# First attention of a fused transformer kernel: output product, shift and two routing calls moved between the two halves of the score rounds

## The chip, the cores and the metric

The kernel runs on one core of one Trainium2 chip. The metric is the device time of one execution in microseconds (us); of several runs the median is taken. A core has five engines that run their own queues and meet at semaphores: TensorE (PE; its weight loads are shown as PEld), VectorE (DVE), ScalarE (ACT), GpSimd (POOL) and SyncE (SP), which issues DMAs here.

## The reference

Two layers, each an attention and a mixture of experts, on x of 64 sequences with 128 rows of 128 numbers, in fp32:

```python
x = x + xattn0(layernorm(x), fside, ctx, ctx)   # 16 heads of 8; 128 + 120 keys
x = x + ffn0(layernorm(x))                       # 8 experts, 2 for each row, logits from a small attention
x = x + xattn1(layernorm(x), ctx, ctx)           # 16 heads; 120 keys
x = x + ffn1(layernorm(x))                       # 8 experts, 2 for each row
```

The first attention is what the change is about. For each sequence and head:

```python
q = (xn @ Wq + bq); k = concat(fside @ Wk + bk, ctx); v = concat(fside @ Wv + bv, ctx)
attn = softmax(q @ k.T * 8 ** -0.5)
out = concat_heads(attn @ v) @ Wp + bp
```

## The kernel before

`attention` (L232 on) is a loop over `it`, one turn for each sequence with five turns to drain (L517). It is a software pipeline: in turn `it`, the score maxima are made for sequence `it`, the exponentials for `it - 2`, the products with the values for `it - 3`, and the output steps for `it - 3` to `it - 5`. Sequences come in groups of four (`GB`); once a group, spread over the four turns, the next group's queries, keys and values are prepared (`prep`).

The steps of a turn of the first attention, with their engines:

- `rounds(0, 1)` and `rounds(2, 3)` (L524, `round_` L413). A round is two banks of maxima (`max_bank`: TensorE at L373, then a DVE reduction at L385) and two banks of scores (`score_bank`: TensorE at L401, then an ACT exponential at L409). Two rounds are one block: eight banks of PSUM[...].
- `shift` (L426): two TensorE transposes of the negated maxima (L430), and two DVE operations that add them to the queries (L433). The scores of a sequence (two turns after its maxima) need its queries shifted.
- `values` (L437): 64 TensorE records at L446, then `out1`, an ACT copy (L455).
- `out2` (L458): two transposes (L462), a DVE reciprocal and product. `out3` (L473): a transpose (L475) and an ACT copy. `out4` (L480): the output product (L482). `out5` (L485): a DVE addition to x (L487) and `aside.made`, the statistics of the next norm (L109).
- `aside.ahead` (L547): the statistics of the first norm for a later sequence, on DVE; with every fourth one POOL makes the roots.
- `aside.call`: one step of the router of the experts (`Router.call`, L612) and of its lists, twice in a turn. The router has three generators: `front` (normed rows on POOL, transposes at L176, logits at L652), `back` (the choice of experts, on DVE, POOL and ACT; ranks by TensorE at L805), `sent` (scatters by POOL, L783). Each says at which call it goes on; most of `back` takes one step in each call, 15 or 16 calls for two groups of sequences.
- `prep(it, half)` (L323), by `it % 4`: turn 0 writes the next group's queries (`prep_q`, a product at L289 and four ACT writes at L293, two in each half); turn 2 its keys (`prep_k`, L202, two ACT writes at L207) and values (`prep_v`, L214, two DVE additions at L221); turn 3 turns the normed rows (`prep_x`, L176).

Every engine of `ORDERED` takes its instructions in the order in which the program writes them (`manual_schedule`). The order of the calls in L540 to L556 is therefore the order on TensorE, DVE, ACT and POOL each. SP's DMAs are not held to it inside this loop.

All PSUM banks come from one pool of eight (`mtile`, L275). A bank goes back when its last reader is done, and the one that has been free longest is handed out next. So about eight banks after a bank is taken, TensorE waits for that bank's reader. `prep_q(g, 0)` takes a bank that `prep_q(g, 1)` reads too; it is not handed out in between.

Of the kernel before, what the change touches and what calls it, by code (L numbers as in the profile page):

```python
# [44 lines left out]
def transformer_kernel(ctx, tc, a, out):  # L45
# [155 lines left out]
    def keys_of(w, src, g, n0, pk):  # L201
        nc.tensor.matmul(  # L202
            pk[:, : GB * n0], lhsT=w["wk"], rhs=src.rearrange("d b k -> d (b k)"),
            start=True, stop=True,
        )
        for v in range(NV):
            nc.scalar.activation(  # L207
                K2[g % 2][:, v, :, 0:n0], pk[:, : GB * n0].rearrange("p (b k) -> p b k", b=GB),
                AF.Identity, bias=w["bk"][:, v : v + 1], scale=kmask[:, v : v + 1],
            )  # L210

    def values_of(w, src, g, n0, pv):
        for j in range(GB):
            nc.tensor.matmul(  # L214
                pv[:n0, j * D : (j + 1) * D], lhsT=src[:, j, :], rhs=w["wv"],
                start=True, stop=True,
            )
        pv5 = pv[:n0, :].rearrange("k (b h i d) -> k b h i d", b=GB, i=2, d=HD)
        bv5 = w["bv"][:n0, :].rearrange("k (h i d) -> k h i d", i=2, d=HD)
        for i in range(2):  # L220
            nc.vector.tensor_tensor(  # L221
                VS[g % 2][0][:n0, :, :, i, 16 * i : 16 * i + HD], pv5[:, :, :, i, :],
                bv5[:, :, i, :].unsqueeze(1).to_broadcast([n0, GB, H // 2, HD]),
                ALU.add,
            )
# [6 lines left out]
    def attention(layer, w, norm, first, aside):  # L232
# [5 lines left out]
        with ExitStack() as es:  # L238
# [13 lines left out]
            def loads(g):  # L252
                n = KF if first else KC
                t = work.tile([D, GB, n], F32, name="kvT", tag="kvT")
                nc.sync.dma_start(t, a["fsideT" if first else "ctxT"][:, g * GB : (g + 1) * GB, :])
                src[g] = t
# [13 lines left out]
            def context(g):  # L270
                if first:
                    context_k(g)
                    context_v(g)

            def mtile():  # L275
                return banks.tile([128, 512], F32, name="bank", tag="bank")

            def prep_x(g):
                xnT = work.tile([D, GB * S], F32, name="xnT", tag="xnT", bufs=1)
                norm.turned(normed.pop(g), mtile(), xnT)  # L280
                xnTs[g] = xnT
                q4s[g] = work.tile([128, GB, NS, S], F32, name="q4", tag="q4", bufs=3)
# [3 lines left out]
            def prep_q(g, v):  # L286
                if v == 0:
                    pqs[g] = mtile()
                    nc.tensor.matmul(pqs[g], lhsT=w["wq"], rhs=xnTs[g], start=True, stop=True)  # L289
                pq = pqs[g]  # L290
                for i in range(2):
                    s = 2 * v + i
                    nc.scalar.activation(  # L293
                        q4s[g][:, :, s, :], pq.rearrange("p (b q) -> p b q", b=GB),
                        AF.Identity, bias=w["bq"][:, s : s + 1], scale=hmask[:, s : s + 1],
                    )

            def prep_k(g):
                keys_of(w, src[g], g, n0, mtile())

            def prep_v(g):
                values_of(w, src[g], g, n0, mtile())
# [20 lines left out]
            def prep(it, half):  # L323

                g, j = it // GB + 1, it % GB
                if not first:
                    if g == 1:
                        if (j, half) == (2, 1):
                            prep_v(1)
                        elif (j, half) == (1, 0):  # L330
                            prep_k(1)
                    elif g < NG:
                        pieces = (
                            (), (lambda: prep_k(g),),
                            (lambda: prep_v(g), lambda: prep_x(g)),
                            (lambda: prep_q(g, 0), lambda: prep_q(g, 1)),
                        )[j]
                        if half < len(pieces):
                            pieces[half]()
                    return  # L340
                if half == 0 and it < GB - 1:
                    prep_batch(it + 1)
                if (it, half) == (0, 1):
                    prep_v(0)
                    norm_of(1)
                if (it, half) == (1, 1):
                    biased(0)
                if (it, half) == (2, 1):
                    prep_x(1)
                if (it, half) == (3, 0):  # L350
                    prep_q(1, 0)
                    prep_q(1, 1)
                if (j, half) == (3, 1):
                    if g + 1 < NG:
                        prep_x(g + 1)
                elif g >= NG:
                    return
                elif j == 0 and it:
                    prep_q(g, half)
                elif (j, half) == (2, 0):  # L360
                    prep_k(g)
                elif (j, half) == (2, 1):
                    prep_v(g)


            def max_bank(b, ra, v):
# [123 lines left out]
            def norm_of(g):  # L490
                if g < NG:
                    normed[g] = norm.normed(g)
                    biased(g)

            def biased(g):

                nc.gpsimd.tensor_tensor(
                    xg[g], xg[g], w["bo"].unsqueeze(1).to_broadcast([S, GB, D]), ALU.add
                )
# [17 lines left out]
            for it in range(B + 5):  # L517
                def on(back, *steps):
                    b = it - back
                    if 0 <= b < B:  # L520
                        for f in steps:
                            f(b)

                def rounds(*which):  # L524
                    ba = it if it < B else None
                    bc = it - 2 if 0 <= it - 2 < B else None
                    for r in which:
                        if ba is not None or bc is not None:
                            round_(ba, bc, r)

                if first and it % GB == 2:
                    norm_of(it // GB + 2)
                if 2 <= it <= B + 1:
                    ps_[it - 2] = work.tile([128, nc_, 4, 512], F32, name="p", tag="p")
                if it % GB == 0 and 0 < it // GB + 1 < NG:
                    if it:
                        loads(it // GB + 1)
                vals = (lambda b: values(b, 0), lambda b: values(b, 1), out1)
                if first:
                    rounds(0, 1)  # L540


                    on(3, *vals)
                    if it % GB == 2 and it // GB + 1 < NG:
                        context(it // GB + 1)
                    on(5, out4, out5)
                    aside.ahead(it)  # L547
                    aside.call(it, mtile)
                    rounds(2, 3)
                    on(1, shift)  # L550
                    on(4, out3)
                    on(3, out2)
                    prep(it, 0)
                    prep(it, 1)
                    aside.call(it, mtile)
                    aside.end(it, work, mtile)  # L556
                else:
                    on(3, *vals)
                    rounds(0, 1)


                    aside.piece(mtile)
                    if it < GB - 1:
                        prep_batch(it + 1)
                    prep(it, 0)
                    on(4, out3)
                    on(3, out2)
                    on(5, out4)
                    aside.call(it, mtile)
                    prep(it, 1)  # L570
                    on(1, shift)
                    on(5, out5)
                    aside.ahead(it)
                    if it == GB - 1 or it > GB and it % GB == 1:
                        norm_of(it // GB + 1)
                    if it == 1:
                        biased(0)
                    if it == GB - 1:
                        prep_x(1)
                        prep_q(1, 0)  # L580
                        prep_q(1, 1)
                    aside.fetch_for(it)
                    aside.call(it, mtile)
                ps_.pop(it - 3, None)
                yield
# [840 lines left out]
```

## Time and profile before

| what | us |
|---|---|
| median of the runs | 1637.03 (1634.42 to 1637.46) |
| the profiled execution | 1538.39, its span 1536.6 |
| busy: PE / DVE / ACT / POOL | 1411.3 / 1064.3 / 842.7 / 642.2 |
| mean granted TensorE clock | 0.978 |
| first attention, first to last product with the values | 36.8 to 626 |
| experts of the first layer | about 640 to 960 |
| second attention and its experts | about 970 to 1536 |

The page lists busy time by engine, the granted clock in 40 slices, the chain of work that ended last, and groups of instructions by line with what ended the idle time before them. An answer on waits names who waited for whom, the total in us, how often, and the longest. A line of the timeline has the start and length in us, the engine, the line of the kernel and what it reads and writes, and in brackets the idle time of the engine ahead of it and who ended it. In windows, the columns after the length are the busy times of PE, PEld, DVE, ACT and POOL with their counts, the granted clock, the DMA share and GB/s. One matmul in fp32 is two records.

### The profile page before, as it was taken

How to read it: one execution, taken by the hardware profiler on the slowest of the kernel's cores; microseconds unless marked ns; L12 is line 12 of the kernel's file. 1: busy time of each engine (PE TensorE's matmuls, PEld its weight loads, DVE VectorE, ACT ScalarE, POOL GpSimd, SP SyncE). 2: the span in 40 equal slices, each digit the busy share in tenths (PEclk: the TensorE clock that was granted, in tenths of full speed). 3: DMA queues.
4: the chain of work that ended last, by engine and by line, in shares of the span. 5: the costliest groups of instructions: out<-in, count | busy, mean ns of one | idle time of the engine just before them, and what ended most of it. 6: DMA issues, size and time to landing. Idle time of an engine off the chain costs nothing.

```text
span 1536.6 us, 44811 instructions
## 1 busy us (share of the span) xinstructions
PE 1411.3 (92%) x18162; PEld 1143.2 (74%) x18162; DVE 1064.3 (69%) x2935; ACT 842.7 (55%) x1739; POOL 642.2 (42%) x1198
## 2 busy tenths in 40 slices
PE   7999999999999899888999998579899999999987
PEld 5777777777777677777888887457777777777765
DVE  7778888888888888454544443358777767777763
ACT  4666666666666665443333332346665666666643
POOL 4123355555565535644000000677754566644110
PEclk9999999999999999999999999589999999999999
DMA  8411122222222221467766665111111111110000
GB/s 209 102 48 48 47 59 61 62 63 62 62 62 61 55 74 35 132 192 213 214 201 186 187 193 156 37 34 29 35 36 29 36 29 41 36 31 16 16 9 28
DMA packets 124128, 123.88 MB, mean 81 GB/s; under 512 B 47123, under 2 KB 106515, under 8 KB 122003
## 3 DMA queue, kind: packets, MB, share of 16 engines
q1 hardware_dynamic: 115730, 103.71, 24.6%
q0 software_dynamic: 8192, 17.32, 3.7%
q8 instruction: 143, 2.34, 0.6%
q14 instruction: 63, 0.51, 0.1%
HBM read 97.31 MB, written 23.67 MB: 79 GB/s over the span
## 4 chain that ended last, share of the span: by engine, by line
PE 62%; DVE 20%; ACT 6%; POOL 4%; DMA 4%; issue 3%; SPq 0%; POOLq 0%; DVEq 0%; ACTq 0%
PE bank L446 10%; PE bank L1029 9%; PE bank L401 8%; PE bank L373 7%; DVE nm L385 6%; PE bank L1283 4%; PE bank L1042 3%; PE bank L1304 3%; ACT q L293 3%; DVE q L433 2%; PE bank L482 2%; DMA q<-xs 2%; DMA vc<-xs 2%; PE bank L202 2%; PE bank L462 2%
## 5 line engine op out<-in xcount | busy, mean ns | idle before, releaser
L385 DVE TENSOR_REDUCE nm<-bank 128x2 f32<-128x496 f32 (+1 forms) x768 | 461.2, 662 | 57.3 <-PE bank L373 32.2
L409 ACT ACTIVATE p<-bank 120x512 f32<-120x512 f32 (+1 forms) x768 | 397.5, 603 | 164.1 <-PE bank L401 146.8
L373 PE MATMUL bank<-k,q 32*128 32x248 f32 (+1 forms) x4096 | 446.2, 341 | 3.5 <-ACT q L318 2.2
L401 PE MATMUL bank<-q,k 32*120 32x256 f32 (+1 forms) x3072 | 417.3, 404 | 21.8 <-ACT q L293 12.7
L373 PEld LDWEIGHTS bank<-k,q 32*128 32x128 f32 x4096 | 351.0, 191 | 47.7 <-DVE nm L385 11.9
L401 PEld LDWEIGHTS bank<-q,k 32*120 32x120 f32 (+1 forms) x3072 | 277.7, 181 | 43.0 <-ACT q L293 18.2
L1034 DVE TENSOR_TENSOR p<-p,bank 128x256 f32<-128x256 f32 x213 | 88.3, 421 | 132.8 <-ACT p L1033 132.8
L446 PE MATMUL bank<-p,v 128*32 128x128 f32 (+1 forms) x4096 | 176.3, 277 | 1.9 <-DVE nm L385 1.9
L783 POOL DMA_INDIRECT xs<-xn,at x128 | 129.3, 1010 | 26.3 <-issue 21.2
L1215 POOL DMA_INDIRECT yb<-ys,back x128 | 124.0, 968 | 32.2 <-issue 25.0
L446 PEld LDWEIGHTS bank<-p,v 128*32 128x32 f32 (+1 forms) x4096 | 109.6, 110 | 36.9 <-issue 24.1
L1033 ACT ACTIVATE p<-bank 128x256 f32<-128x256 f32 x213 | 81.0, 384 | 98.8 <-PE bank L1029 98.8
L1029 PE MATMUL bank<-q 128*128 128x256 f32 x516 | 118.6, 379 | 0.8 <-ACT q L1020 0.8
L433 DVE SCALAR_TENSOR_TENSOR q<-bank,c_smask,q 128x256 f32<-128x256 f32 x256 | 111.2, 476 | 10.7 <-PE bank L430 8.1
L167 POOL TENSOR_SCALAR xn<-x,mv,rstd 128x128 f32<-128x128 f32 x252 | 110.9, 452 | 11.6 <-issue 5.5
L455 ACT COPY ov<-bank 128x256 f32<-128x256 f32 x128 | 47.9, 375 | 104.2 <-PE bank L446 101.6
L293 ACT ACTIVATE q<-bank,c_a_bq,c_hmask 128x512 f32<-128x512 f32 x120 | 85.4, 780 | 34.2 <-PE bank L289 34.2
L1201 POOL MEMSET gates<- 128x256 f32 x2 | 0.6, 312 | 246.8 <-DMA ys<-q 246.8
L1029 PEld LDWEIGHTS bank<-q 128*128 128x128 f32 x516 | 94.7, 190 | 12.1 <-ACT q L1020 1.0
L446 PE MATMUL bank<-p,vc 120*32 120x128 f32 x2048 | 103.2, 272 | 0.0
L155 POOL TENSOR_SCALAR rstd<-mv 128x4 f32<-128x4 f32 (+1 forms) x33 | 6.6, 199 | 201.4 <-DVE mv L113 114.6
L487 DVE TENSOR_TENSOR x<-x,bank 128x128 f32<-128x128 f32 x128 | 36.2, 282 | 71.8 <-PE bank L482 70.3
(205 smaller groups left out, 2332.2 us busy)
## 6 DMA issues: line engine op xcount, KB each, us to landing
q<-in_w SPq DMA_DIRECT2D x43, 576.0 KB, 4.5
vc<-in_w SPq DMA_DIRECT2D x28, 576.0 KB, 3.9
vc<-in_ctx_v SPq DMA_DIRECT2D x16, 960.0 KB
k<-in_ctx_k SPq DMA_DIRECT2D x32, 240.0 KB, 2.7
q<-xs SPq DMA_DIRECT2D x43, 128.0 KB, 2.2
ys<-q SPq DMA_DIRECT2D x43, 128.0 KB, 3.4
x<-in_x SPq DMA_DIRECT2D x16, 256.0 KB, 5.0
kvT<-in_fsideT SPq DMA_DIRECT2D x16, 256.0 KB
```

Source lines behind the costliest of these rows:

```text
L167: nc.gpsimd.tensor_scalar(xn[:, j, :D], xg[g][:, j, :], self.mv[:, b, 0:1], self.rstd[:, b : b + 1], ALU.add, ALU.mult,)
L293: nc.scalar.activation(q4s[g][:, :, s, :], pq.rearrange("p (b q) -> p b q", b=GB), AF.Identity, bias=w["bq"][:, s : s + 1], scale=hmask[:, ...
L373: nc.tensor.matmul(pa[:, u, :], lhsT=q4s[g][r, j, s, :], rhs=k2[g % 2][r, s // 2, j, :], start=True, stop=True,)
L385: nc.vector.tensor_reduce(nm[b % 2].rearrange("q i (a s) -> q a i s", s=16)[:, 2 * ra + v : 2 * ra + v + len(slots) // 2, :, 0], pa.rearra ...
L401: nc.tensor.matmul(pb[:n, v * 256 : (v + 1) * 256], lhsT=k2[g % 2][r, v, j, k0 : k0 + n], rhs=q4s[g][r, j, 2 * v : 2 * v + 2, :].rearrange ...
L409: nc.scalar.activation(ps_[b][:n, c, ra, :], pb[:n], AF.Exp, scale=SCALE)
L433: nc.vector.scalar_tensor_tensor(q, pm, smask[:, v : v + 1], q, ALU.mult, ALU.add)
L446: nc.tensor.matmul(pav[32 * ra : 32 * ra + 32, v * S : (v + 1) * S], lhsT=vs[g % 2][c][:, j, 4 * v + ra, i, :], rhs=p[:n, c, ra, (2 * v + ...
L783: s = nc.gpsimd.indirect_dma_start(xs, bass.IndirectOffsetOnAxis(at[:, j, k : k + 1], 0), xn, None)
L1029: nc.tensor.matmul(ph[:, u, :], lhsT=w[:, c, u * 128 : (u + 1) * 128], rhs=xT, start=True, stop=True)
L1034: nc.vector.tensor_tensor(hT[:, c, :], sa, ph[:, 1, :], ALU.mult)
L1215: nc.gpsimd.indirect_dma_start(y[:, k, b % 2, :], None, ys, bass.IndirectOffsetOnAxis(back[:, b, k : k + 1], 0),)
```

## The change

In the first attention's turn:

- `out4`, `shift`, `out5`, `aside.ahead` and the first `aside.call` come straight behind `rounds(0, 1)`, ahead of the values.
- `prep(it, 0)` and the second `aside.call` come ahead of `rounds(2, 3)`. With turn 0 of a group this is half of the queries' writes, with turn 2 the values.
- Behind `rounds(2, 3)` stay `out3`, `out2`, `prep(it, 1)` and `aside.end`.
- Keys and values of a group change places: the values are made in the first half of turn 2, the keys in the second.

```diff
                 elif j == 0 and it:
                     prep_q(g, half)
                 elif (j, half) == (2, 0):
+                    prep_v(g)
+                elif (j, half) == (2, 1):
                     prep_k(g)
-                elif (j, half) == (2, 1):
-                    prep_v(g)
...
                     rounds(0, 1)
 
 
+                    on(5, out4)
+                    on(1, shift)
+                    on(5, out5)
+                    aside.ahead(it)
+                    aside.call(it, mtile)
                     on(3, *vals)
                     if it % GB == 2 and it // GB + 1 < NG:
                         context(it // GB + 1)
-                    on(5, out4, out5)
-                    aside.ahead(it)
+                    prep(it, 0)
                     aside.call(it, mtile)
                     rounds(2, 3)
-                    on(1, shift)
                     on(4, out3)
                     on(3, out2)
-                    prep(it, 0)
                     prep(it, 1)
-                    aside.call(it, mtile)
                     aside.end(it, work, mtile)
```

In the first three turns `prep(it, 0)` also prepares the first group's next sequence (`prep_batch`), and in turn 3 both halves of the second group's queries; these move with it.

## The prediction

> **What bounds the kernel now.** I read the page first (busy shares, granted clock), then the busy time by windows, the waits, and the timeline of a few turns of the loop (a turn is one value of it). From the page and the windows, for turns 32 to 39:
>
> ```profile
> PE 1411.3 (92%) x18162; PEld 1143.2 (74%) x18162; DVE 1064.3 (69%) x2935; ACT 842.7 (55%) x1739; POOL 642.2 (42%) x1198
> ```
>
> ```profile
> 305.69:381.40 75.71, 71.53 (x1146) 55.79 (x1148) 63.53 (x163) 48.72 (x99) 43.35 (x96) 1.00 0.24 63
> ```
>
> Eight turns take 75.7 us with TensorE at full clock and busy 94%, DVE 84%. So TensorE is the bound, and what can be won is only its pauses. The waits between 200 and 500 us (total, times, longest):
>
> ```profile
> PEld bank L430 <- DVE nm L385: 18.2, 31, 0.9
> PEld bank L401 <- ACT q L293: 10.9, 8, 1.4
> PE bank L401 <- ACT q L293: 7.8, 8, 1.0
> PEld bank L446 <- DVE nm L385: 4.4, 12, 0.4
> PEld bank L401 <- DVE lg L656: 1.9, 4, 0.5
> PE bank L401 <- DVE q L433: 0.6, 4, 0.2
> ```
>
> These are waits for a free bank (L385, L293 and L656 read banks) or for shifted queries (L433). The timeline shows two of them:
>
> ```profile
> 300.76 2.42 DVE L385 TENSOR_REDUCE nm<-bank 128x2 f32<-128x496 f32 x4 [0.22 <-PE bank L401]
> 300.81 2.07 ACT L409 ACTIVATE p<-bank 120x512 f32<-120x512 f32 x4 [0.56 <-PE bank L401]
> 302.88 0.68 PE L373 MATMUL bank<-k,q 32*128 32x248 f32 x2
> 303.10 0.87 DVE L433 SCALAR_TENSOR_TENSOR q<-bank,c_smask,q 128x256 f32<-128x256 f32 x2
> 303.72 0.45 PE L401 MATMUL bank<-q,k 32*128 32x256 f32 x1 [0.16 <-DVE q L433]
> ...
> 307.58 0.49 PE L482 MATMUL bank<-c_a_wo,oT 128*128 128x128 f32 x2
> ...
> 311.95 0.68 PE L373 MATMUL bank<-k,q 32*128 32x248 f32 x2
> 312.06 2.79 ACT L293 ACTIVATE q<-bank,c_a_bq,c_hmask 128x512 f32<-128x512 f32 x4 [0.65 <-PE bank L289]
> 314.90 0.48 PE L401 MATMUL bank<-q,k 32*128 32x256 f32 x1 [0.97 <-ACT q L293]
> ```
>
> At 302.88 the next turn's first block starts, but its scores need the shift (L433), which DVE does only after four reductions: 0.8 us lost. At 314.90 the eighth bank of a first block is the one that prep_q's four writes (2.79 us) still read: 2 us lost.
>
> **Durations, off the timeline.** From one operation's start on TensorE to the next one's: a block of two rounds 1.91; values 1.89; out4 0.33 (0.42 ahead of a block); shift 0.27, out3 0.17, out2 0.27 (0.36 ahead of a block); prep_q 0.95; prep_k 0.86 (0.95 ahead of a block); prep_v 0.98; turned 0.52; router logits (L652) 0.90; prep_x 0.53; ranks (L805) 0.47. Counted from a block's start, reductions begin at 1.13 and end at 1.81, 2.39, 2.97, 3.55; exponentials run from 1.18 to 3.25. DVE: shift 0.87, out5 with stats 0.8, out2 0.54. A block stopped at its eighth bank needs 1.05 from its release to the next operation (the rest after 314.90, values at 315.95).
>
> *Test on before.* For a group of four turns without routing steps (turns 8 to 11) this arithmetic gives 9.99, 8.85, 9.04 and 8.33, sum 36.2; the starts of the values (81.8, 91.8, 100.7, 109.7, 118.0) give 10.0, 8.9, 9.0, 8.3. With routing the trace has 75.7/2 = 37.8: its DVE steps, right ahead of the reductions, cost 1.7 a group.
>
> **The change, turn by turn.** Each number is from one out4 to the next.
> - *Removed:* the wait for L433 (0.5 to 0.8 in three of four turns): the shift now lies half a turn ahead of its use. Removed too: the 2 us at 314.90 in its present form.
> - *Behind the second block* only out3 and out2 stand now (0.8 with the way to the next block), where shift, prep and a call gave DVE and ACT time to drain eight banks. This is what is late next.
> - *Turn 0 (mod 4):* out4, shift, values, prep_q: 3.65 to the second block. prep_q's bank stays taken until its second half, behind that block, so seven banks serve eight: the eighth waits for the first reduction (1.86), out3 comes at 2.9 and the next block at 3.4. Its eighth bank is prep_q's: ACT ends oT at 3.85, two writes (1.40) at 5.25, and out4 follows at 6.3. Sum 9.95 (before 10.0): one stall of 2 us has become two of 1 us.
> - *Turn 1:* 3.92 with turned and logits; the next block's third bank needs the third reduction (3.0 against 2.46), next out4 at 4.95. Sum 8.87 (before 8.86).
> - *Turn 2:* prep_v ahead costs 3.65. prep_k at the end: its matmul ends at 3.5, two ACT writes (0.77 each, L207) at 5.05, but its bank is the eighth of the next block, reached at 4.46; out4 at 6.12. Sum 9.77 (before 8.98). A new stall, the swap's price.
> - *Turn 3:* 2.67; prep_x, then a wait for the fourth reduction, 5.39. Sum 8.06 (before 8.31).
>
> Group: 36.65 against 36.2, **0.5 lost** without routing.
>
> *Routing.* Both calls now lie in the first half, behind shift and stats. There DVE has 1.2 us (turn 3) to 2.5 us (turn 1) before the second block's reductions, and the two calls take up to 1.65 (four selection steps 0.92, three more 0.7). In turns 0 and 1 they fit; in turn 2 prep_v and a call of 0.9 overrun (0.5 once in eight). New waits: once in eight turns the rank matmuls (L805) need sums that DVE makes in the call just ahead: 0.8, with values, the next block and all behind it queued on TensorE. Router logits need ACT's xnT copy; values (1.89) hide it; without that cover it would be 0.6. POOL's steps keep their order; its scatters (about 1.0 each, L783) wait on nothing new, and SP's loads of context stay behind values: nothing. So routing costs 0.6 a group in place of 1.7: 36.65 + 0.6 = 37.3 against 37.8, **0.5 won**.
>
> *Sum.* 3 groups without routing: +1.5. 11 with: -5.5. The last turns, without prep: 8.3 becomes 7.6, five times: -3.5. Start: DVE waited there for blocks held up by a late shift (24.71, after a wait of 2.5 for L433): -2.5, bounded by 0 and -4. Together **-10 us**: the profiled execution (span 1536.6, 1538.4 in all) would come to 1528. The runs' median is 1637.0, 99 us more, and nothing in the profile says where that lies; I carry the difference over as it is: 1627 (scaled by 1637/1538 it would be -10.6).
>
> [...]
>
> **Rivals.**
> - *A, slower, 0.38:* the bank that ACT reads at a turn's end (prep_q's in turn 0, prep_k's in turn 2) is the next block's eighth in my working, as at 314.90. If it comes up earlier in the block or ACT gets there later, TensorE stands up to 1.1 us longer, 29 times. From 0.35 us on average it eats the 10 us; at 0.8 it is +23 - 10 = +13: **1650**. For it: nothing but out2 lies between these reads and the block. Against it: banks come free in order, and these are last.
> - *B, nothing, 0.12:* the routing steps do cost as much as before, since each now waits for POOL or ACT of the call just ahead (POOL steps of 1.07 to 1.27 us, L732 to L740). Then 14 groups at +0.5, less the 6 at both ends: +1, **1638**.
> - *C, forecast, 0.50:* **1627**; with the two stalls of turn 0 overlapping, down to 1612.
>
> **Numbers.** Within 0.2% (3.3 us) is about what a measurement of this kernel can tell from no change. Faster 0.50, same 0.12, slower 0.38. The range takes in C's lower end and A: 1610 to 1654.
>
> **What would show it.** Right: no wait of L401 for L433; L430 hardly waiting; waits for L293 in both blocks of turns 0 and 1, about 0.5 us each; a new wait for L207 ahead of turn 3; L805 waiting for DVE; turns of 9.9, 8.9, 9.8, 8.1 plus routing. Wrong: L385 or L409 starting late in second blocks by over 1 us (FIFO), waits for L207 or L293 above 1.5 us (A), a clock below 1.00 between 100 and 490 us, or a gap elsewhere than before 640 us.

## The result, and the profile after

The changed kernel takes 1627.92 us (median, 1626.05 to 1632.96) against 1637.03 us of the kernel before (1634.36 to 1639.27) on the same chip, nine runs each: a ratio of 0.9949, interval 0.9937 to 0.9961. That is 9 us faster. The profiled execution took 1627.08 us, its span 1625.1.

The runs fell on several chips. By the median of the kernel before on each they are of two kinds: 1637.03 to 1638.72 us in three comparisons (the slower kind), 1540.16 to 1540.88 in four (the quicker). The comparison above was made on the slower kind; the profile of before that the prediction works from is, by its time (1538.39), of the quicker. So the traces of before and after can't be set side by side: the 88 us between their spans have the other sign than the change. Each experiment is therefore compared, as a ratio, with runs of the kernel before on its own chip, and the traces compared below are b1 (before, run again) and a1 (after, run again), both from the quicker kind.

The page of the changed kernel, with its row of the granted TensorE clock:

```profile
PE 1489.3 (92%) x18162; PEld 1184.0 (73%) x18162; DVE 1072.5 (66%) x2935; ACT 842.1 (52%) x1739; POOL 642.3 (40%) x1198
...
PEclk9999999999999998999999996799998989899999
```

The instructions are the same in number (18162, 2935, 1739, 1198), as they should be where steps are only moved; PE's busy time rose by 78 us without any added work. The clock row shows one reason (mean granted clock 0.954, against 0.978 in the trace of before): eights in slices 31, 33 and 35 (from 1219 us on), in the second attention, which the change doesn't touch, and one in slice 16 (from 609 us on), at the end of the first. Two windows of the same profile, eight turns of the first attention and 100 us of the second (the third last number is the granted clock):

```profile
310.30:386.70 76.40, 74.85 (x1141) 56.79 (x1140) 64.60 (x163) 48.40 (x99) 43.42 (x95) 1.00 0.24 62
1130.00:1230.00 100.00, 92.94 (x1163) 73.50 (x1162) 64.89 (x193) 55.20 (x107) 54.69 (x81) 0.91 0.10 29
```

The waits that answer to those of before, 200 to 500 us (total, times, longest):

```profile
PEld bank L401 <- DVE nm L385: 8.2, 20, 0.7
PEld bank L475 <- DVE nm L385: 6.7, 20, 0.4
...
PEld bank L401 <- ACT k L207: 2.2, 6, 0.4
...
PEld bank L401 <- ACT q L293: 1.7, 8, 0.2
```

Gone are the 18.2 us of L430 and the wait of L401 for L433; the wait for the queries' writes (L293) fell from 10.9 to 1.7 us on the weight loads and is 0.2 at most, where 0.5 was expected and 1.4 had been the longest; the keys' writes (L207) are new. This much is as the prediction had it. Yet eight turns take 76.40 us here against 75.71 before, at a clock of 1.00. In four turns of this profile (26, 34, 42 and 50) ACT's copy of the products with the values starts 1.98 to 2.00 us after the last of them, where 0.34 is usual; that is 1.65 us each, which no trace of the quicker chips has in this attention.

### The profile page after: what moved, and what is told of

It is laid out like the page before. It is cut to its first block, busy times and chain, and to the rows that moved or that the text cites. A ratio compares the mean times of both kernels' runs of the same rounds, so it can differ in the third digit from the quotient of the medians.

```text
span 1625.1 us, 44888 instructions
## 1 busy us (share of the span) xinstructions
PE 1489.3 (92%) x18162; PEld 1184.0 (73%) x18162; DVE 1072.5 (66%) x2935; ACT 842.1 (52%) x1739; POOL 642.3 (40%) x1198
## 4 chain that ended last, share of the span: by engine, by line
PE 74%; DVE 11%; DMA 4%; issue 3%; ACT 3%; POOL 3%; SPq 1%; another core or an unknown queue 0%; POOLq 0%; DVEq 0%; ACTq 0%
PE bank L401 13%; PE bank L373 12%; PE bank L1030 9%; PE bank L446 9%; PE bank L1305 4%; PE bank L1284 3%; DVE nm L385 3%; PE bank L1043 3%; PE bank L289 2%; DMA q<-xs 2%; PE bank L1294 2%; PE bank L482 2%; PE bank L202 2%; PE bank L214 2%; PE bank L653 2%
## 5 line engine op out<-in xcount | busy, mean ns | idle before, releaser
L401 PE MATMUL bank<-q,k 32*120 32x256 f32 (+1 forms) x3072 | 480.4, 408 | 16.8 <-issue 5.6
L373 PE MATMUL bank<-k,q 32*128 32x248 f32 (+1 forms) x4096 | 466.0, 345 | 11.1 <-issue 7.5
L409 ACT ACTIVATE p<-bank 120x512 f32<-120x512 f32 (+1 forms) x768 | 402.4, 603 | 138.0 <-PE bank L401 102.8
L373 PEld LDWEIGHTS bank<-k,q 32*128 32x128 f32 x4096 | 355.5, 191 | 80.4 <-issue 32.9
L401 PEld LDWEIGHTS bank<-q,k 32*120 32x120 f32 (+1 forms) x3072 | 302.2, 181 | 47.2 <-DVE nm L385 16.1
L1030 PE MATMUL bank<-q 128*128 128x256 f32 x516 | 122.3, 388 | 3.0 <-ACT oT L477 3.0
L433 DVE SCALAR_TENSOR_TENSOR q<-bank,c_smask,q 128x256 f32<-128x256 f32 x256 | 111.2, 476 | 14.2 <-PE bank L430 10.9
L293 ACT ACTIVATE q<-bank,c_a_bq,c_hmask 128x512 f32<-128x512 f32 x120 | 87.3, 785 | 47.7 <-PE bank L289 47.7
L138 POOL TENSOR_TENSOR mv<-st 128x4 f32<-128x4 f32 x31 | 6.4, 207 | 195.4 <-DVE st L109 195.4
```

Source lines behind the costliest of these rows:

```text
L293: nc.scalar.activation(q4s[g][:, :, s, :], pq.rearrange("p (b q) -> p b q", b=GB), AF.Identity, bias=w["bq"][:, s : s + 1], scale=hmask[:, ...
L373: nc.tensor.matmul(pa[:, u, :], lhsT=q4s[g][r, j, s, :], rhs=k2[g % 2][r, s // 2, j, :], start=True, stop=True,)
L401: nc.tensor.matmul(pb[:n, v * 256 : (v + 1) * 256], lhsT=k2[g % 2][r, v, j, k0 : k0 + n], rhs=q4s[g][r, j, 2 * v : 2 * v + 2, :].rearrange ...
L409: nc.scalar.activation(ps_[b][:n, c, ra, :], pb[:n], AF.Exp, scale=SCALE)
L433: nc.vector.scalar_tensor_tensor(q, pm, smask[:, v : v + 1], q, ALU.mult, ALU.add)
L1030: nc.tensor.matmul(ph[:, u, :], lhsT=w[:, c, u * 128 : (u + 1) * 128], rhs=xT, start=True, stop=True)
```

## The experiments

In the expectations T is my theory at that point (at first the prediction's own: what counts is how long TensorE stands for a bank whose reader is late), and the other letters are rivals told there. Where they give microseconds, these are on the scale of the 1627.9 above, so I compare ratios; "to a1" is a ratio divided by a1's.

**b1: the kernel before, unchanged**, to get its trace from the chip of the first experiments.

> The kernel before, unchanged, for a profile that belongs to the timed executions: the one shown before spans 1536.6 us, the runs take 1637. Theory T (the loop's pauses): first attention, from the first to the last product with the values, takes some 10 us more than in the changed kernel's profile (37.4 to 640), and the second attention takes as long as there (about 600). Rival H (granted clock): first attention ends by 626 as in the profile shown, and the whole difference of 9 us lies behind it, in windows of half clock (the changed kernel's profile shows 22 stretches at 0.50, 16 of them after 1000 us).

Measured: 1539.39 us (its median there 1540.88). The trace is the one of before again: first product with the values at 37.3, last one of the first attention at 625.8, of the second 1485.0. The half clock (granted 0.50) in it takes 7 us up to the end of the first attention. At the change of layers stands one long stretch of it (31 to 44 us, in every trace); behind that, b1 has 22 us.

**swap_back: keys and values of a group in their old order.**

```diff
                 elif (j, half) == (2, 0):
-                    prep_v(g)
+                    prep_k(g)
                 elif (j, half) == (2, 1):
-                    prep_k(g)
+                    prep_v(g)
```

> The changed kernel with keys in the first half of turn 2 and values in the second, as in the order before. By the sums of the prediction (T): at the end of turn 2, two DVE additions hold the eighth bank instead of two ACT writes (free at 5.0 instead of 5.05 from the block's start), so turn 2 changes by under 0.1; but once in eight turns the wait of about 1 us for the bank of the values in the first half goes: 1624, range 1620 to 1629. Rival A (the keys' bank at the turn's end is what costs): 0.8 a group, 1616 to 1618.

Measured: 1535.54 us, 0.9964 [0.9950, 0.9979]; to a1 0.998, 3 us. Turn 2 became 9.66 in place of 9.79, or of 10.02 once in eight; but the turn with ranks became 9.35 in place of 8.78. In two groups with routing that cancels: 28.67 us for the two turns 2 and the turn with ranks, against 28.59 in a1. The last product comes 2.2 us earlier, mostly by turn 54 (9.66 in place of 12.01). So the swap costs 3 us at most, not the 11 us that the rival A needs.

**shift_late: shift behind the second half again, all else as changed.**

```diff
-                    on(5, out4)
-                    on(1, shift)
-                    on(5, out5)
+                    on(5, out4, out5)
...
                     rounds(2, 3)
+                    on(1, shift)
```

> The changed kernel with the shift behind the second block, as before. T: the scores of the next block wait for L433 again, 0.7 in turn 1, 0.3 in turn 3, 0 in turns 0 and 2 (hidden behind ACT's banks), 0.7 in the turns without prep: 1644, range 1638 to 1650. Rival B (the shift's place is worth nothing, since the next block waits for its banks anyway): 1626 to 1630.

Measured: 1545.32 us, 1.0027 [1.0013, 1.0042]; to a1 1.0045, 7 us slower. Its waits, 200 to 500 us:

```profile
PEld bank L430 <- DVE nm L385: 8.1, 24, 0.4
...
PEld bank L401 <- DVE q L433: 7.1, 8, 0.9
```

The wait of the scores for the shifted queries is back, so the mechanism is the one named; its size is about half of what T gave.

**call_late: the second routing call behind the second half again.**

```diff
                     prep(it, 0)
-                    aside.call(it, mtile)
                     rounds(2, 3)
...
                     prep(it, 1)
+                    aside.call(it, mtile)
                     aside.end(it, work, mtile)
```

> The changed kernel with the second router call at the end of the turn, as before. T: the rank matmuls no longer wait (0.8 in eight turns) and the logits fill the pause at the end of turn 1 (0.5 in four), but the DVE steps come between second block and the next block's reductions, which were just in time (0.3 to 0.7 later in turns 1 and 3): 1630, range 1622 to 1638. Rival B (two calls side by side cost): 1615 to 1621, from 2 us in eight turns.

Measured: 1519.44 us, 0.9861 [0.9843, 0.9879]; to a1 0.988, 18 us, beyond what T and B gave, and faster than both kernels. Turn 1 went from 9.19 to 8.47 (8.9 to 9.1 once in eight), the turn with ranks from 8.78 to 8.04, and the late turn 2 from 10.02 to 9.79. Router logits (L652 before, L653 here) and ranks (L805, L806 here) are TensorE's own work, 0.9 and 0.5 us. In the first half they lengthen their turn, by 0.72 and 0.74 us; behind the second block TensorE stands for the reductions anyway, and they fill the pause.

**a1: the changed kernel, unchanged**, on the next chip.

> The changed kernel, unchanged, beside the others of this study and on the chip that the kernel before does 1541 us on. If the ratio of the first comparison (0.9949) belongs to the change, it comes out at 0.995, 1533. The two runs that undo a part (0.9964 with keys and values back, 1.0027 with the shift back) put it between 0.993 and 0.998. The changed kernel's profile shows four turns in which the last product with the values is reported 1.65 us late, and 90 us of half clock after 1000 us, the six others none and 22 to 26. Theory H (a state of the chip on which that profile was taken): neither is there in this profile, first attention ends near 623, second attention takes near 540. Theory C (the change makes them): both are there, and the ratio is near 1.03.

Measured: 1537.36 us against 1540.21, 0.9982 [0.9972, 0.9992] (22 and 28 runs). Its clock row, and the same 100 us of the second attention as above:

```profile
PEclk9999999999999999999999999589999999999999
```

```profile
1130.00:1230.00 100.00, 97.08 (x1376) 77.93 (x1372) 76.85 (x227) 64.53 (x125) 57.45 (x87) 1.00 0.12 33
```

The same program, and the clock stays at 1.00 where it was 0.91; half clock behind the change of layers takes 22 us, not 94; there is no late copy in the first attention. So both belong to the chip or to that execution, not to the change. And here the change is worth 3 us, not 9.

**q_end: both halves of the queries' writes behind the second block.**

```diff
                 elif j == 0 and it:
-                    prep_q(g, half)
+                    if half:
+                        prep_q(g, 0)
+                        prep_q(g, 1)
```

> The changed kernel with both halves of the queries' writes behind the second block. T: turn 0 has one stall of about 2 us instead of two of 1: 10.15 by the prediction's arithmetic against 10.38 measured: 0.2 a group, 0 to -4 us against the changed kernel. Rival D (the seven banks of the split halves cost a stall that the whole does not have): turn 0 at 9.5 or less, -12 us or more.

Measured: 1550.26 us, 1.0063 [1.0039, 1.0087]; to a1 1.0081. Both expectations missed. Its waits (200 to 500 us; L403 is L401 of the other kernels) and two windows:

```profile
PEld bank L403 <- ACT q L293: 13.5, 8, 1.7
...
PE bank L403 <- ACT q L293: 10.4, 8, 1.3
```

```profile
460.00:500.00 40.00, 38.13 (x579) 29.10 (x572) 33.16 (x82) 25.32 (x53) 19.53 (x44) 0.96 0.23 62
500.00:540.00 40.00, 35.20 (x540) 27.18 (x540) 33.65 (x94) 21.36 (x44) 22.91 (x50) 0.96 0.20 53
```

The one long stop is back (up to 1.7 us where a1 has 0.2), and turn 0 takes 10.5 to 11.05 from values to values, at full clock, where a1's takes 10.38. What nobody expected is the clock: 31 us at half speed up to the end of the first attention, against 7 in b1. Six of the stretches begin 1.2 to 1.9 us behind such a stop, as at 480.19 and 521.15, in the two windows. The kernel before has one long stop in a group as well; there TensorE itself (the PE line) pauses for 0.97 us, here for 1.30.

**q_twice: call_late, and the second half of the queries from a product made again in turn 3's first half.**

```diff
-                if v == 0:
+                if v == 0 or first and g > 1:
                     pqs[g] = mtile()
...
-                    prep_q(g, half)
+                    if half == 0:
+                        prep_q(g, 0)
+                elif (j, half) == (3, 0) and it > 3:
+                    prep_q(g, 1)
```

> call_late, with the queries' second half written in turn 3's first half from a product of its own (repeated, 0.95 us of TensorE a group), so that no bank is held across the second block and none of its writes stands ahead of the next block. T (turn 0's length is the two bank stalls): turn 0 falls from 10.38 to 8.6, turn 3 grows from 8.04 to 9.0: -0.8 a group, 12 us off call_late, ratio to before 0.978, 1507. Rival E (turn 0 is long from the product and ACT's load, not from the banks): turn 0 stays above 9.8 and the whole is 5 to 10 us slower than call_late.

Measured: 1529.48 us, 0.9935 [0.9913, 0.9958]: 0.7% slower than call_late. Turn 0 fell from 10.38 to 9.3 or 9.9, but turn 3 rose from 8.04 to 9.15, more than the product repeated. And the stop in turn 0 stayed (L404 is L401 of the other kernels):

```profile
125.29 1.45 ACT L293 ACTIVATE q<-bank,c_a_bq,c_hmask 128x512 f32<-128x512 f32 x2 [0.66 <-PE bank L289]
...
126.79 0.17 PEld L404 LDWEIGHTS bank<-q,k 32*120 32x120 f32 x1 [0.44 <-ACT q L293]
```

The bank that ACT reads at 125.29 comes up in the second block after all, 0.4 us before ACT is done with it. T had looked only at the bank that was held across the block.

**best: call_late, with keys and values in the old order and the start's queries behind the second half.** In the first turns `prep(3, 0)` also writes all four parts of the second group's queries; the edit moves them.

```diff
-                if (it, half) == (3, 0):
+                if (it, half) == (3, 1):
                     prep_q(1, 0)
                     prep_q(1, 1)
...
                 elif (j, half) == (2, 0):
-                    prep_v(g)
+                    prep_k(g)
                 elif (j, half) == (2, 1):
-                    prep_k(g)
+                    prep_v(g)
```

> call_late with two more edits: keys in the first half of turn 2 and values in the second, and in turn 3 the four writes of the second group's queries behind the second block instead of ahead of it. T: turn 2 falls from 9.79 to about 9.65 (measured in swap_back), 2 us in all; in turn 3 the four writes (2.79 us on ACT) no longer stand ahead of the second block's exponentials, 1 to 2 us once: ratio 0.984 (0.982 to 0.986 from call_late's 0.986). Rival: with the second call at the turn's end, the values' additions and the routing steps together delay the next block's reductions, and turn 2 is 9.8 or more: ratio 0.987 to 0.990.

Measured: 1519.40 us, 0.9864 [0.9845, 0.9883]: no gain over call_late (0.9861) that can be measured, though the trace shows a part of what T said: turn 2 at 9.66 to 9.72. From the first to the second product with the values it takes 9.88 us, but call_late takes 10.03, so the four writes are worth 0.15 us and not 1 to 2. The last product comes at 605.3 where call_late has 607.5; 1.5 us of that stand ahead of the first one, where call_late has 6.8 us at half clock and this run 3.4.

**b2 and b3: the kernel before, unchanged**, for its trace on the slower kind of chip.

> The kernel before once more, for its profile on the chip that this call runs on. On a chip that does it in 1541 us, the same profile as b1. On a chip that does it in 1637 us, theory H says that its first attention is longer than 626 us by about as much as the changed kernel's profile of there (642) exceeds a1's (622.6), and that half clock takes about 90 us after 1000 us.

> The kernel before, unchanged, on whatever chip this call gets. If it is one that does it in about 1638 us (as the first comparison's and shift_only's), theory H expects half clock of about 90 us after 1000 us, as in the changed kernel's profile of there, and a first attention longer than 626; its length against the changed kernel's 604.7 from first to last product with the values (37.4 to 642.1) then says how much of the 9 us lies in the loop. If it is one of 1541 us, the same as b1 and b2.

Measured: 1539.55 and 1540.74 us, both on the quicker kind. Half clock behind the change of layers is 22 us in each.

**shift_only: the kernel before with shift alone moved**, behind out4 and ahead of out5, so behind the values.

```diff
                     on(3, *vals)
...
-                    on(5, out4, out5)
+                    on(5, out4)
+                    on(1, shift)
+                    on(5, out5)
                     aside.ahead(it)
                     aside.call(it, mtile)
                     rounds(2, 3)
-                    on(1, shift)
```

> The kernel before with one edit: the shift directly behind out4, ahead of out5 and the first call. T: the waits of L401 for L433 go (by the prediction's arithmetic turn 1 falls from 8.9 to 8.4, turn 2 from 9.0 to 8.7, turn 3 from 8.3 to 8.0, turn 0 stays at 10.0: 1.0 a group without routing), but DVE now has 0.4 us instead of 1.0 before the second block's reductions, so routing steps cost up to 0.5 more in six of eight turns: ratio to before between 0.990 and 1.000. Rival (the early shift only pays together with the moved calls and preparations): 1.000 or more.

Measured: 1666.74 us against 1638.72, 1.0153 [1.0119, 1.0188]: T is wrong, the rival holds. Waits of 200 to 500 us, then two lines of DVE in turn 10:

```profile
DVE q L433 <- PE bank L430: 47.6, 29, 3.3
```

```profile
105.55 0.88 DVE L433 SCALAR_TENSOR_TENSOR q<-bank,c_smask,q 128x256 f32<-128x256 f32 x2 [1.14 <-PE bank L430]
...
107.05 2.40 DVE L385 TENSOR_REDUCE nm<-bank 128x2 f32<-128x496 f32 x4
```

Shift stands at the head of DVE's queue and waits for transposes that TensorE reaches only behind 1.9 us of values; out5, the statistics and then the second block's reductions queue behind it. Turns 8 to 11 sum to 37.0 in place of 36.1, turns 16 to 21, with routing, to 61.9 in place of 58.3, all at full clock. So an early shift does not pay behind the values; ahead of them it was run only with the calls moved too.

**kv_late: call_late, keys and values both behind turn 2's second half, the start's queries behind turn 3's.**

```diff
-                if (it, half) == (3, 0):
+                if (it, half) == (3, 1):
...
-                elif (j, half) == (2, 0):
-                    prep_v(g)
                 elif (j, half) == (2, 1):
                     prep_k(g)
+                    prep_v(g)
```

> call_late with the keys and then the values of turn 2 both behind the second block, as before the change, and the writes of turn 3 of the start behind it too. T (what stands between the second block and the next one is free time for DVE and ACT to drain the banks): turn 2 falls from 9.79 to about 8.9 (two products of 0.86 and 0.98 fill a pause that is there anyway, and the keys' bank is free before it is asked for): 0.9 a group, ratio to before 0.978 (0.976 to 0.981 from call_late's 0.986). Rival (turn 2 is long from ACT's and DVE's load, wherever the products stand): 9.6 or more, ratio 0.985 to 0.988.

Measured: 1601.13 us against 1638.02 (the slower kind), 0.9771 [0.9745, 0.9797], as expected. Turn 2 fell from 9.79 to 8.97 to 9.03; over 15 groups that is 12 us, 0.8%, about what the ratio shows. call_late was not run on the slower kind, where the change alone has a ratio lower by 0.0033, so the ratios by themselves don't prove the step from 0.986. By its turns it is the best version of these.

## Why the prediction was right, and where its steps were not

The predicted 1627 stands a microsecond from the measured 1627.92. The agreement is mostly luck: the sum of -10 was worked out on a trace of the quicker kind, where the medians of before and changed kernel differ by 3 (0.9982), and carried unscaled to the slower kind, where they differ by 9. Step by step on b1 and a1, us over the whole first attention (start to third product with the values, then by stretches of turns):

| step | predicted | measured |
|---|---|---|
| start | -2.5 | +2.3 |
| groups without routing | +1.5 | +1.75 |
| groups with routing | -5.5 | -5.3 (turns 16 to 51: -3.7; 52 to 59: -1.6) |
| last turns | -3.5 | -2.0 |
| sum | -10 | -3.2 (last product at 622.6, was 625.8) |

**The waits that go, and the groups: right, but for turn 1.** In a1 TensorE waits neither for L433 nor at L430 between 200 and 500 us. Turns 8 to 11, out4 to out4, are 9.94, 9.19, 9.79 and 8.04; worked out were 9.95, 8.87, 9.77 and 8.06. Their sum is 36.96 against 36.14 in b1: 0.8 lost, where 0.5 was worked out. That three such groups still come to 1.75 is because the first of them (turns 5 to 7) loses nothing. With routing, two groups take 74.89 against 75.64 in b1, so 0.4 a group is won; 0.5 was worked out. The timeline of a1 shows the new small stops:

```profile
315.32 1.47 ACT L293 ACTIVATE q<-bank,c_a_bq,c_hmask 128x512 f32<-128x512 f32 x2
316.84 0.18 PEld L401 LDWEIGHTS bank<-q,k 32*128 32x128 f32 x1 [0.22 <-ACT q L293]
...
331.69 0.21 ACT L713 ACTIVATE e<-e 128x8 f32<-128x8 f32 x1 [1.55 <-DVE e L712]
...
334.33 1.45 ACT L207 ACTIVATE k<-bank,c_a_bk,c_kmask 128x512 f32<-128x512 f32 x2 [0.21 <-PE bank L202]
335.82 0.18 PEld L401 LDWEIGHTS bank<-q,k 32*128 32x128 f32 x1 [0.35 <-ACT k L207]
```

At 316.84 and 335.82 TensorE waits at the eighth bank for ACT's two writes, in turn 0 for the queries and ahead of turn 3 for the keys, where the prediction put them.

**Turn 1, mis-sized:** 9.19, not 8.87. The second block begins on time (3.97 behind out4, worked out 3.92), but the next out4 comes 5.22 later, not 4.95: the pause behind a block that is packed with only out3 and out2 is 0.3 longer than the reductions' end times gave.

**The start, the step that failed:** "-2.5, bounded by 0 and -4" was +2.3. The wait of 2.6 us for L433 is gone, but the first product with the values comes no earlier (37.48, b1 37.31): TensorE now waits at that place for reductions (0.53 and three times 0.29 us between 24.2 and 26.0) and later for the keys' writes (0.56). So waits that were hidden behind the old one take its place. Of the +2.3, 0.6 is only the values' later place in the turn. The rest is turn 3: `prep(3, 0)` writes the second group's queries in four parts, and these now stand ahead of the second block, whose banks ACT must drain too. In a1, and then in call_late:

```profile
40.54 2.79 ACT L293 ACTIVATE q<-bank,c_a_bq,c_hmask 128x512 f32<-128x512 f32 x4 [0.66 <-PE bank L289]
...
43.38 0.47 PE L401 MATMUL bank<-q,k 32*120 32x256 f32 x1 [1.39 <-ACT q L293]
...
44.00:50.00 6.00, 6.00 (x78) 4.59 (x77) 4.09 (x8) 4.03 (x8) 0.00 (x0) 0.72 0.48 116
```

```profile
44.70 0.47 PE L401 MATMUL bank<-q,k 32*120 32x256 f32 x1 [1.39 <-ACT q L293]
...
44.00:50.00 6.00, 5.30 (x94) 4.26 (x98) 4.17 (x9) 5.25 (x10) 0.00 (x0) 1.00 0.76 178
```

From the first to the second product with the values a1 takes 11.66 us and b1 9.88; best and kv_late, which move these writes back, take 9.88 again. But call_late and swap_back, which leave the writes where they are and have the same stop of 1.39 us, take 10.03. So the writes themselves cost 0.15 us. The other 1.6 is the clock: a1 has a stretch of 3.41 us at half clock from 45.1 on (granted 0.72 over the window), and call_late has none there. The prediction counted the late shift that goes and missed the four writes that come, which the change's own description named, and its sum has no term for the clock.

**The last turns** gave 2.9 from out4 to out4, 3.5 was worked out; by the values, which now stand later in a turn, 2.0. Counted by out4 to the end, the start is -0.2 and the turns from 60 on give 0.0: how much falls to the two ends depends on where one cuts.

**The routing steps: right in the loop, with one part not foreseen.** DVE's routing steps were charged only where they overrun its time ahead of the second block's reductions: in turn 2, "0.5 once in eight". That DVE had time to spare there was read off the trace of before, where it sits idle 0.73 us for out4 at 299.74 and again at 308.11. The trace of a1 agrees: the overrun comes once in eight turns, and costs 0.23. In turns 14, 22, 30, 38 and 46 (10.02 in place of 9.79) the values' additions wait 1.08 us at the head of DVE's queue for their product, the call's reduction stands behind them, and the second block's reductions start 5.0 us behind out4 in place of 4.76; the prediction's sign against itself ("FIFO", in its last lines) was a delay of over 1 us. Turn 38:

```profile
368.52 0.76 DVE L221 TENSOR_TENSOR v<-bank,c_a_bv 128x256 f32<-128x256 f32 x2 [1.08 <-PE bank L214]
369.20 0.68 DVE L735 TENSOR_REDUCE r<-pp 128x64 f32<-128x512 f32 x1
369.79 2.41 DVE L385 TENSOR_REDUCE nm<-bank 128x2 f32<-128x496 f32 x4
```

The wait at 331.69 above looks worse and costs nothing: a small exponential of the choice of experts (L713) waits 1.55 us for DVE at the head of ACT's queue, but its turn takes 9.79. The wait of the ranks for DVE that was foreseen did not come (at most 0.4 us ahead of L806, put down to issue); that turn is 0.74 longer all the same, 0.5 of it the ranks' own time. Of the -1.6 in turns 52 to 59, up to 1.7 is the clock and not the routing: b1 has its one stretch at half clock in the loop there (3.41 us from 503.66 on; 1.7 is half of it, an estimate), and a1 has none. What the prediction did not look for is that TensorE's own part of the calls could have stayed in the pause: call_late is 18 us faster than a1.

**The clock: as expected in the loop, not at the start.** The sum has no term for it, and the sign against the prediction, a clock below 1.00 between 100 and 490 us, did not come: between 50 and 600 us a1 has no half clock at all. At the start it has the stretch at 45.1, above. Between 40 and 640 us the 14 traces have 26 stretches at half clock, and 24 of them begin in or within 2.6 us behind a pause of TensorE (no product running) of 1.19 us or more. There are 85 such pauses, so most of them are not followed by one. Of the 53 pauses of 0.9 to 1.1 us, most of them the kernel before's long stop (0.97), none is. The start's stop of 1.39 was followed by a stretch in a1, q_end, q_twice and the first profile of the changed kernel, and not in call_late, swap_back and shift_late; why in some and not in others isn't shown.

**Rivals.** A (the bank comes up earlier) did not come: the waits for L293 and L207 stay at 0.2 to 0.4 us. B (nothing) is closer to a1's 3 us than the forecast is, but not for B's reason, since the groups with routing did win.

**What stays open.** Why the same change wins 9 us on one kind of chip and 3 on the other. There is no profile of the kernel before on the slower kind, so where the other 6 us lie there isn't shown. For the changed kernel the two traces can be compared: of the 92 us between their spans, 19.5 lie in the first attention, 9 between it and the second, 63 behind. In the first attention 6 of the 19.5 are the four late copies, and 9 are turn 65, whose copy comes 5.57 us after the last product. kv_late, on another chip of that kind, has the same in its turn 65 (5.47). In turns 23, 31, 39 and 47 its values take 3.25 us from the first product to the last, in place of 1.70, with pauses of TensorE for nothing that the profile names (issue); shift_only, on a third, has 2.92 to 3.55 in the same four. In the traces of the quicker kind no copy in this attention is late, and values are long only at half clock. The cause isn't shown. The 99 us that "nothing in the profile says where" are in part the clock: in the three profiles from the slower kind, half clock behind the change of layers takes 87 to 101 us, against 22 to 26 on the quicker one. At half speed, 70 us more of it cost about 35 (an estimate, if TensorE is the bound there); the rest is open.

## What to carry to other kernels

Between two blocks that each fill all eight banks of the pool the engines that drain them need time (in a1 TensorE waits 9.0 us at L401 and 8.1 at L475 for the reductions, between 200 and 500 us): put TensorE's other products into that pause (the gain of call_late and kv_late, 0.986 and 0.977), and not into the half that TensorE already fills. A step moved earlier paid here where the engine that does it gets there without waiting: shift ahead of the values, with the calls moved too, won 7 us; behind the values, in the kernel before, it cost 1.5%. When a step is moved, list every branch that moves with it, those of the first turns too: here the start took back 2.3 of the 5.5 us that the loop and the last turns won, 1.6 of it by a stretch at half clock (3.41 us) that a1 has behind the stop of 1.39 us at four moved writes, and call_late has not.

## What the runs showed of the hardware that was not expected

- The kernel before took 1540.16 to 1540.88 us (medians) on four chips and 1638.02 and 1638.72 on two. The granted clock of the profiled executions was 0.972 to 0.980 on the one kind and 0.945 to 0.954 on the other; behind the change of layers half clock took 22 to 26 us on the one and 87 to 101 on the other.
- In the traces of the two kernels (before, and the first profile of the changed one) every stretch at half clock, but for the one that the span's end cuts, is one to eleven times 3.41 us long. Of the 26 stretches that the 14 traces have between 40 and 640 us, 24 begin in or within 2.6 us behind a pause of TensorE of 1.19 us or more (counted above; no run tests the cause). The queries' writes in one stop of 1.30 us a group (q_end) were followed by six stretches; in one of 0.97 (b1), or in short stops of 0.2 to 0.4 us (a1), by none.
- A block that stopped at its eighth bank needed 1.05 us from the bank's release to the next operation (before, 314.90 to 315.95). So a short wait at that place costs more than it shows: in a1 the block at 314.94 takes 2.96 us, the one at 321.88, without a stop, 1.91, and the wait shown is 0.22.
- On the slower kind of chip the values or the copy behind them lose 1.2 to 1.9 us in a turn of each eight, at full clock (turns 26, 34, 42 and 50 of one chip, 23, 31, 39 and 47 of two others); no trace of the quicker kind has that.
